# Two fused attention blocks on one core: the seven stores of a prepared weight leave two a step, ahead of a gather

## The chip, the core and the metric

The kernel runs on one NeuronCore of a Trainium2 chip. The metric is the device time of one execution in microseconds (us), of which lower is better. The core has five engines, each with an instruction stream of its own: TensorE (PE), VectorE (DVE), ScalarE (ACT), GpSimd (POOL) and SyncE (SP). SP does no arithmetic here: it issues nearly all transfers between the chip's DRAM and on-chip memory. POOL issues those that add while they move.

## What is computed

Two attention blocks follow each other on x of shape (8, 512, 32, 32) in 32-bit floats; the weights of the two differ. One block, for one batch element with 512 channels C and 1024 positions:

```python
xn = group_norm(x)                       # 8 groups, then gamma and beta
q, k, v = wq @ xn + bq, wk @ xn + bk, wv @ xn + bv     # 512x512 weights
attn = softmax(q^T k * 64 ** -0.5)       # 8 heads of 64 channels, 1024 x 1024
out = x + wp @ (attn v) + bp
```

## The kernel before, in words

**Jobs.** A job is one block on one batch element. There are 16, in the order batch 0 block 0, batch 1 block 0, batch 0 block 1, batch 1 block 1, then the next two batches in the same way. I call them job 0 to job 15. A job has two stages on PE. In the attention, 8 groups (a pair of heads by half of the queries) of 8 steps each follow each other: step i computes one block of scores (`sc`, L1102) and, two steps behind, multiplies an earlier block of exponentials with v (`po`, L1153). In the projections, the output projection of the finished job and v, k and q of the next one are computed (L804, L809; after job 0 the simpler L556 as well).

**Products with seven multiplications.** A matrix product is split in 2x2 blocks and done with seven block products, each on sums of blocks; most projections do this at two levels. The sums of the activations are DVE's work between the attention's steps: L426 to L432 make the sums `t` of xn, and L485 to L491 the second level, in a tile named `deep` (first four steps from xn, last four from `t`). The sums of the weights are made once. For the attention output's and v's weights that is `deep_round`: it loads four raw blocks into a tile `round`, makes four sums of 512 elements a partition and four of 896 with DVE (L165 to L171), and stores seven results of 448 KB each to DRAM (L155). It runs once in each of jobs 0, 1, 2 and 3 (`ROUNDS`). Jobs 0 and 1 also prepare the first level for k and q (`FIRST`, function `put_first`): four loads into a tile `raw`, four sums (again L165 to L171), and two stores to a DRAM tile `keep`. The tiles `round`, `raw` and `deep` take turns in one buffer: the next may be filled only when everything that reads the last, its stores included, is done.

**The softmax's sums.** ACT computes the exponentials `e` (L1107). They are added up by DVE (L1121, L1123), and in most groups the first four of a group go in pairs: POOL issues a transfer that adds one `e` to another (L1130), and DVE adds that sum some steps later (L1133). A sum over partitions follows (r, L1188). After two groups, SP gathers the parts of r (L1211), DVE inverts (lt, ri, rt, L1215 to L1235), SP sends the reciprocals to DRAM (rd, L1228) and back to all partitions (rb, L1230), and DVE multiplies (L1245). Groups also end with a copy-out of `po` (L1174 on ACT, L1176 on DVE). The 12 buffers of `e` serve in the projections for the weights `w`, which SP loads (L192, L198).

**What sets the order.** PE, ACT and DVE run in the order in which the program writes their instructions; transfers marked by `in_turn` keep their place in SP's order. An engine's instruction that waits holds up all that follow it on this engine. In the loop of `run`, each step i issues its scores, values, pair addition, and then what stands under i in two tables: `chores` (DVE work, entered by `put`) and `moves` (mostly transfers, entered by `move`). Both take the next free step if one is taken. A clock that counts planned time (`advance`) starts what `later` has put off, the gather and the inversion among them. In `put_round`, the seven stores go into `moves` from step 26 on at the next free steps, up to the thirties; the gather of r for groups 2 and 3 is issued at about step 34, in between.

Of the kernel before, what the change touches and what calls it, by code (L numbers as in the profile page):

```python
# [54 lines left out]
ROUNDS = {0: (O, 0), 1: (V, 1), 2: (O, 1), 3: (V, 0)}  # L55
# [26 lines left out]
def fast_path(  # L82
# [36 lines left out]
    def advance(us):  # L119
        clock[0] += us  # L120
        due = sorted((t for t in todo if t[0] <= clock[0]), key=lambda t: t[0])
        for t in due:
            todo.remove(t)
            t[1]()
# [956 lines left out]
    class Attention:  # L1081
# [171 lines left out]
            for at, step in zip(times, (gather, invert, spread, normalise)):  # L1253
                later(at, step)

        def run(self, chores, moves, taken=False):


            steps = self.steps
            self.add(1)  # L1260
            self.add(2)
            self.values(0)
            for at in (chores, moves):
                if 2 in at:
                    at[2]()
            for i in range(3, len(steps) + LEAD):
                if i < len(steps):
                    self.scores(i)
                self.values(i - LEAD)
                g, kc = steps[i - LEAD]  # L1270
                if kc % 2 == 1 and kc < 2 * self.pairs(g):
                    self.add_pair(i - LEAD)
                if i in self.due:
                    self.due.pop(i)()
                if kc == NT - 1:
                    if taken and g + 1 == len(self.groups):
                        self.reduce(g)
                    else:
                        self.finish(g)
                    advance(0.85)  # L1280
                for at in (chores, moves):
                    if i in at:
                        at[i]()
                advance(1.71)
# [258 lines left out]
    for n in range(-1, len(jobs)):  # L1543
        last = n + 1 == len(jobs)
        outs = None
        if n >= 0:
            chores, moves = {}, {}

            def put(i, fn):
                while i in chores:  # L1550
                    i += 1
                chores[i] = fn
                return i

            def move(i, fn):
                while i in moves:
                    i += 1
                moves[i] = fn
                return i

            def put_round(which, layer):
                load, first, second, stores = deep_round(which, layer)
                begin = {0: 6, 1: 12}.get(n, 9)
                move(begin, load)
                at = begin + 3
                for fn in first:
                    at = put(at + 1, fn)
                for fn in second:
                    at = put(at + 1, fn)
                at = max(at + 3, 25)  # L1570
                for i, fn in enumerate(stores):
                    at = move(at + 1 + i % 2, fn)

            def put_first(which, layer):
                at = move(37 if n == 0 else 2, lambda: start()) + 3
                box = []

                def start():
                    box.append(acts.tile([P, NW, 2, CH], F32, tag="deep", name=f"raw_{n}"))
                    load_blocks(box[0], layer, which)  # L1580

                for part in range(4):
                    at = put(at + 1, lambda part=part: factor(box[0], part))
                move(at + 1, lambda: store_factors(box[0], layer, which))

            if last:
                w = last_weights(n)
                for part in range(4):
                    put(12 + 2 * part, lambda part=part: factor(w, part))
                for i, fn in enumerate(last_sums(0)):  # L1590
                    put(49 + 3 * i, fn)
            else:
                for i, (_, fn) in enumerate(extra):
                    put(2 + i, fn)
                if n == 1:
                    at = (8, 14, 15, 16, 17, 18, 17, 19, 20, 21)
                else:
                    for i, fn in zip((3, 3, 4, 5, 5, 6, 7, 7, 8), reads):
                        put(i, fn)
                    at = (16, 22, 23, 24, 26, 27, 29, 31, 33, 35)  # L1600
                    if n < DEEP_V + 2:
                        at = (17, 24, 26, 27, 29, 30, 31, 32, 33, 34)
                for i, fn in zip(at[:2], steps):
                    put(i, fn)
                for i, fn in zip(at[2:], steps[2:]):
                    move(i, fn)
                if n == 1:
                    put_first(*FIRST[n])
                for i, fn in zip(at[len(steps) :], sums(n + 1)):
                    put(i, fn)  # L1610
                if n in ROUNDS:
                    put_round(*ROUNDS[n])
                if n == 0:
                    put_first(*FIRST[n])
                put(52 if n in ROUNDS else 48, lambda q=att.q: out_combine(q, None, 0))
                deep_first = deep_steps(n + 1)
                if n + 1 >= DEEP_V:
                    for i, fn in enumerate(deep_first):
                        put(37 + 2 * i if n not in ROUNDS else ((39, 40, 41, 43, 45, 47, 49, 50) if n == 1 else (36, 37, 38, 40, 41, 43, 45, 47))[i], fn)
                else:  # L1620
                    for at, fn in zip((47, 48, 49, 50), deep_first[4:]):
                        put(at, fn)
                move(58, lambda: extend_plan(n + 1))
                for _ in range(RING):
                    move(58, fetch)
            assert max([*chores, *moves], default=0) < NT * len(att.groups) + LEAD
            if n + 1 >= DEEP_V and not last:
                outs = OutputSums(n)
                ahead = deque()
                if jobs[n][1] == 1 and jobs[n][0] + 2 < B:  # L1630
                    ahead.extend(load_steps(jobs[n][0] + 2))
                both, plan_sums = deep_phases(n + 1, ahead, outs)

                att.run(chores, moves, True)
                extra = ahead
                plan_sums()
                banks(0, "one")
                if n + 2 < len(jobs):
                    reads, steps = norm_steps(n + 2)
                att.take(len(att.groups) - 1, both[0])  # L1640
                banks(1, "one")
                for thunk in both[1:]:
                    thunk()
                banks(0, "two")
                att = Attention(n + 1)
                att.scores(0)
                att.scores(1)
                banks(1, "two")
                att.scores(2, "po")
                continue  # L1650
            att.run(chores, moves)
            banks(0, "one")
            banks(1, "one")
            if last:
                for i, fn in enumerate(last_sums(1)):
                    later(7.1 + 0.8 * i, fn)
                later(13.0, judge)
                for sh in range(2):
                    last_proj(n, w, sh)
                break  # L1660
            outs = OutputSums(n)
            out_sums(n, outs)
            first = v_phase(n + 1, ORDER)
            for thunk in first[:-1]:
                thunk()
            rest = first[-1:]
            extra = deque()
            if jobs[n][1] == 1 and jobs[n][0] + 2 < B:
                extra.extend(load_steps(jobs[n][0] + 2))
            if n == 0:  # L1670
                load, bias_steps = make_out_bias(1)
                extra.append((8, load))
                extra.extend((11, fn) for fn in bias_steps)
            if n + 2 < len(jobs):
                reads, steps = norm_steps(n + 2)
                if n + 2 <= DEEP_V:
                    extra.extend((15, fn) for fn in reads)
        both, _ = deep_phases(n + 1, extra, outs, deep_first[:4] if outs else ())
        both[0]()
        rest[0]()  # L1680
        if n < 0:
            later(22.0, lambda: load_x(1))
        for thunk in both[1:]:
            thunk()
        banks(0, "two")
        att = Attention(n + 1)
        att.scores(0)
        att.scores(1)
        banks(1, "two")
        att.scores(2, "po")  # L1690
# [249 lines left out]
```

## Time and profile before

| | |
|---|---|
| median of 3 runs | 3184.72 us (3181.73 to 3185.78) |
| the profiled execution | 3183.33 us |
| its span, first to last instruction | 3181.6 us |
| PE, DVE, ACT, POOL busy | 99%, 83%, 73%, 9% of the span |
| granted PE clock, mean | 0.998 |
| instructions | 62172 |
| DMA | 450.31 MB, 142 GB/s on average |

All readings come from the one profiled execution, in us from the first instruction. A line of a timeline gives the start, the length, engine, source line and operation, the tile written and the tiles read, how many such instructions are merged, and in brackets the idle time before it and what ended it. SPq is SP's queue of transfers; the time there is that of issuing. PE is matrix multiplication, PEld the loading of its weights.

### The profile page before, as it was taken

The numbers are of one execution on the slowest core, as the hardware profiler recorded it, in microseconds if no ns is written. First come the engines' busy times: TensorE is split into PE (matmuls) and PEld (weight loads), VectorE is DVE, ScalarE is ACT, GpSimd is POOL, SyncE is SP. The second block draws the span as 40 slices with busy tenths as digits, with TensorE's granted clock in tenths as the row PEclk, the third lists the DMA queues.
The fourth block names the chain that finished last, engine by engine and source line by source line (L and its number), as shares of the span: only waits on it lengthen the run. The fifth ranks groups of instructions, "written<-read, shape, count | busy, mean of one in ns | idle before, by whom it ended". The sixth has DMA issues, their size and how long they took to land.

```text
span 3181.6 us, 62172 instructions
## 1 busy us (share of the span) xinstructions
PE 3154.0 (99%) x24093; PEld 1875.9 (59%) x24093; DVE 2636.2 (83%) x3571; ACT 2332.2 (73%) x4233; POOL 281.0 (9%) x318
## 2 busy tenths in 40 slices
PE   9999999999999999999999999999999999999999
PEld 8366384563846639466393764837548375573844
DVE  8896898978879788797978969789697887978867
ACT  6648687686877868777686776867768687686864
POOL 0100101011010010100001000010000100001000
PEclk9999999999999999999999999999999999999999
DMA  7555575565735455355554545446456463444733
GB/s 276 140 151 158 137 223 125 149 189 122 240 76 147 117 117 160 75 152 159 144 184 87 158 100 138 125 95 179 131 137 181 90 194 72 130 127 95 222 75 82
DMA packets 186190, 450.31 MB, mean 142 GB/s; under 512 B 37928, under 2 KB 54176, under 8 KB 185888
## 3 DMA queue, kind: packets, MB, share of 16 engines
q1 hardware_dynamic: 137040, 296.82, 27.6%
q0 software_dynamic: 48848, 149.44, 25.8%
q8 instruction: 192, 3.15, 0.4%
q14 instruction: 110, 0.90, 0.1%
HBM read 247.41 MB, written 48.17 MB: 93 GB/s over the span
## 4 chain that ended last, share of the span: by engine, by line
PE 94%; DVE 2%; DMA 2%; issue 1%; ACT 1%; SPq 0%; DVEq 0%; ACTq 0%
PE sc L1102 26%; PE po L1153 26%; PE vd L809 11%; PE zd L809 11%; PE yd L809 5%; PE ud L809 4%; PE vd L804 4%; PE zd L804 3%; PE ud L804 1%; PE yd L804 1%; PE z L556 1%; DVE acc L1123 1%; DMA w<-deep 1%; DMA x<-p 0%; ACT e L1107 0%
## 5 line engine op out<-in xcount | busy, mean ns | idle before, releaser
L1107 ACT ACTIVATE e<-sc 128x1024 f32<-128x1024 f32 x1024 | 1044.2, 1025 | 572.0 <-PE sc L1102 547.8
L1102 PE MATMUL sc<-q,k 64*64 64x512 f32 x8192 | 1058.1, 589 | 0.3 <-ACT e L1107 0.2
L1153 PE MATMUL po<-e,v 64*64 64x512 f32 x8192 | 1057.5, 589 | 0.1
L1153 PEld LDWEIGHTS po<-e,v 64*64 64x64 f32 x8192 | 312.7, 133 | 566.6 <-issue 541.4
L1102 PEld LDWEIGHTS sc<-q,k 64*64 64x64 f32 x8192 | 310.9, 133 | 563.8 <-issue 508.9
L1123 DVE TENSOR_TENSOR acc<-acc,e 128x1024 f32<-128x1024 f32 x320 | 389.5, 1217 | 38.8 <-ACT e L1107 28.4
L1130 POOL DMA_DIRECT2D e<-e x224 | 192.9, 861 | 1756.6 <-ACT e L1107 1362.1
L1121 DVE TENSOR_TENSOR acc<-e,e 128x1024 f32<-128x1024 f32 x128 | 156.4, 1222 | 144.8 <-ACT e L1107 144.7
L1133 DVE TENSOR_TENSOR acc<-acc,e 128x1024 f32<-128x1024 f32 x224 | 272.4, 1216 | 1.8
L809 PE MATMUL zd<-deep,w 128*128 128x256 f32 x860 | 240.2, 379 | 0.0
L809 PE MATMUL vd<-deep,w 128*128 128x256 f32 x804 | 223.5, 379 | 0.0
L809 PEld LDWEIGHTS zd<-deep,w 128*128 128x128 f32 x860 | 163.3, 190 | 22.4 <-ACT ud L504 0.2
L809 PEld LDWEIGHTS vd<-deep,w 128*128 128x128 f32 x804 | 152.8, 190 | 20.8
L1188 DVE TRANSPOSE_TENSOR_REDUCE r<-acc 128x32 f32<-128x1024 f32 x128 | 159.4, 1245 | 4.3
L904 POOL DMA_DIRECT2D x<-p x61 | 72.9, 1195 | 981.0 <-ACT p L826 409.1
L851 DVE TENSOR_TENSOR p<-p,s 128x512 f32<-128x512 f32 x185 | 127.2, 688 | 23.8 <-ACT p L826 18.4
L804 PE MATMUL vd<-w,deep 128*128 128x128 f32 x840 | 120.3, 277 | 1.2 <-ACT ud L504 1.2
L851 DVE TENSOR_TENSOR q<-q,s 128x512 f32<-128x512 f32 x64 | 44.2, 691 | 86.8 <-ACT q L828 45.1
L804 PE MATMUL zd<-w,deep 128*128 128x128 f32 x728 | 107.8, 277 | 1.5 <-ACT ud L504 1.5
L804 PEld LDWEIGHTS vd<-w,deep 128*128 128x128 f32 x840 | 107.0, 193 | 1.9 <-ACT ud L504 1.8
L809 PE MATMUL vd<-os,w 128*128 128x256 f32 x364 | 105.5, 379 | 0.0
L809 PE MATMUL zd<-os,w 128*128 128x256 f32 x356 | 99.0, 379 | 1.7 <-ACT yd L500 1.7
(296 smaller groups left out, 4825.4 us busy)
## 6 DMA issues: line engine op xcount, KB each, us to landing
w<-deep SPq DMA_DIRECT2D x399, 448.0 KB, 5.5
e<-e POOLq DMA_DIRECT2D x224, 512.0 KB, 4.7
x<-p POOLq DMA_DIRECT2D x61, 512.0 KB, 6.5
rb<-rd SPq DMA_DIRECT2D x96, 256.0 KB, 3.9
x<-x_dram SPq DMA_DIRECT2D x28, 512.0 KB, 6.0
out_dram<-x SPq DMA_DIRECT2D x28, 512.0 KB, 5.6
deep<-w SPq DMA_DIRECT2D x28, 448.0 KB, 5.9
deep<-round SPq DMA_DIRECT2D x28, 448.0 KB, 9.0
```

Source lines behind the costliest of these rows:

```text
L804: nc.tensor.matmul(ps[:, tokens], moving[i][:, tokens], lhs[:, FACTOR[i], :], start=(start and ti == 0), stop=True, skip_group_check=True,)
L809: nc.tensor.matmul(ps, lhs[:, FACTOR[i], :], moving[i], start=start, stop=True, skip_group_check=True,)
L851: nc.vector.tensor_add(to_, to_, five.to_broadcast([P, 2, QT]))
L904: nc.gpsimd.dma_start(to_, p(part), accum_op=ALU.add)
L1102: nc.tensor.matmul(sc[h * HD : (h + 1) * HD, j, :], k[r, hp, k0 : k0 + HD], q[r, hp, sh * HALF : (sh + 1) * HALF], start=True, stop=True,)
L1107: nc.scalar.activation(e, sc, AF.Exp, scale=SCALE)
L1121: nc.vector.tensor_add(acc[g], self.es[i - 1], e)
L1123: nc.vector.tensor_add(acc[g], acc[g], e)
L1130: nc.gpsimd.dma_start(self.summed[i], self.summed.pop(i - 1), accum_op=ALU.add)
L1133: nc.vector.tensor_add(self.acc[g], self.acc[g], self.summed.pop(i))
L1153: nc.tensor.matmul(po[g][j * HD : (j + 1) * HD, h, :], v[r, kc, d0 : d0 + HD], e[r, j, :], start=(kc == 0), stop=(kc == NT - 1),)
L1188: nc.vector.tensor_reduce(self.r[:, 0, m, :], self.acc.pop(g).rearrange("p j (b e) -> p (j b) e", e=RP), AX.X, ALU.add, apply_transpose=True,)
```

## The change

The stores get a table of their own, `leaving`, which is read last in each step: two stores a step, in steps 27 to 30 (three pairs and a single one) where the sums are ready by step 26. Steps of `leaving` aren't pushed on by other work. In the built program SP has all seven stores ahead of the gather of groups 2 and 3 in jobs 0 to 3; before, three of them (four in job 1) followed it. Apart from that SP's order is the same.

In job 0 the loads of `raw` are entered at step 35 and not 37, and its four sums by that much sooner; the four `deep` sums from `t` at 46 to 49 and not 47 to 50. In job 1 the eight `deep` sums for the next job are entered at 37, 38, 39, 40, 42, 44, 46, 48 and not at 39, 40, 41, 43, 45, 47, 49, 50. On DVE the order of instructions changes in these two places alone. PE, ACT and POOL keep their order, and no instruction is added or removed.

```diff
--- before.py
+++ after.py
@@ -1253,14 +1253,15 @@
             for at, step in zip(times, (gather, invert, spread, normalise)):
                 later(at, step)
 
-        def run(self, chores, moves, taken=False):
+        def run(self, chores, moves, leaving, taken=False):
 
 
             steps = self.steps
             self.add(1)
             self.add(2)
             self.values(0)
-            for at in (chores, moves):
+            tables = (chores, moves, leaving)
+            for at in tables:
                 if 2 in at:
                     at[2]()
             for i in range(3, len(steps) + LEAD):
@@ -1278,7 +1279,7 @@
                     else:
                         self.finish(g)
                     advance(0.85)
-                for at in (chores, moves):
+                for at in tables:
                     if i in at:
                         at[i]()
                 advance(1.71)
@@ -1544,7 +1545,7 @@
         last = n + 1 == len(jobs)
         outs = None
         if n >= 0:
-            chores, moves = {}, {}
+            chores, moves, leaving = {}, {}, {}
 
             def put(i, fn):
                 while i in chores:
@@ -1567,12 +1568,12 @@
                     at = put(at + 1, fn)
                 for fn in second:
                     at = put(at + 1, fn)
-                at = max(at + 3, 25)
-                for i, fn in enumerate(stores):
-                    at = move(at + 1 + i % 2, fn)
+                at = max(at, 26)
+                for i in range(4):
+                    leaving[at + 1 + i] = lambda part=stores[2 * i : 2 * i + 2]: [fn() for fn in part]
 
             def put_first(which, layer):
-                at = move(37 if n == 0 else 2, lambda: start()) + 3
+                at = move(35 if n == 0 else 2, lambda: start()) + 3
                 box = []
 
                 def start():
@@ -1616,9 +1617,9 @@
                 deep_first = deep_steps(n + 1)
                 if n + 1 >= DEEP_V:
                     for i, fn in enumerate(deep_first):
-                        put(37 + 2 * i if n not in ROUNDS else ((39, 40, 41, 43, 45, 47, 49, 50) if n == 1 else (36, 37, 38, 40, 41, 43, 45, 47))[i], fn)
+                        put(37 + 2 * i if n not in ROUNDS else ((37, 38, 39, 40, 42, 44, 46, 48) if n == 1 else (36, 37, 38, 40, 41, 43, 45, 47))[i], fn)
                 else:
-                    for at, fn in zip((47, 48, 49, 50), deep_first[4:]):
+                    for at, fn in zip((46, 47, 48, 49), deep_first[4:]):
                         put(at, fn)
                 move(58, lambda: extend_plan(n + 1))
                 for _ in range(RING):
@@ -1631,7 +1632,7 @@
                     ahead.extend(load_steps(jobs[n][0] + 2))
                 both, plan_sums = deep_phases(n + 1, ahead, outs)
 
-                att.run(chores, moves, True)
+                att.run(chores, moves, leaving, True)
                 extra = ahead
                 plan_sums()
                 banks(0, "one")
@@ -1648,7 +1649,7 @@
                 banks(1, "two")
                 att.scores(2, "po")
                 continue
-            att.run(chores, moves)
+            att.run(chores, moves, leaving)
             banks(0, "one")
             banks(1, "one")
             if last:
```

## The prediction

> **What bounds the kernel now.** I read the page first, then the stages, then what PE waited for, then the two queues behind those waits.
>
> The page's first part:
>
> ```profile
> PE 3154.0 (99%) x24093; PEld 1875.9 (59%) x24093; DVE 2636.2 (83%) x3571; ACT 2332.2 (73%) x4233; POOL 281.0 (9%) x318
> ```
>
> PE is idle for only 3181.6 - 3154.0 = 27.6 us. The change adds no work and removes none; the built programs have the same instructions on every engine, and PE, ACT and POOL have them in the same order. So it can only win time that PE loses. Where that is shows in the attentions of jobs 0 to 4, cut at the first score matmul and at the first matmul after it (columns: stretch, length, busy time of PE, PEld, DVE, ACT, POOL, clock, DMA share, GB/s):
>
> ```profile
> 79.76:191.65 111.89, 110.19 (x1026) 38.82 (x1025) 95.09 (x124) 73.81 (x77) 13.84 (x15) 1.00 0.61 146
> 284.65:398.65 114.00, 110.56 (x1025) 38.90 (x1025) 93.45 (x112) 73.83 (x77) 12.59 (x15) 1.00 0.58 144
> 486.63:598.12 111.49, 110.11 (x1026) 39.10 (x1025) 96.23 (x119) 73.81 (x77) 13.45 (x15) 1.00 0.56 127
> 687.43:801.83 114.40, 110.33 (x1025) 38.99 (x1025) 97.20 (x120) 73.71 (x77) 13.47 (x15) 1.00 0.55 129
> 888.97:999.00 110.03, 110.03 (x1026) 39.03 (x1025) 92.92 (x113) 73.13 (x76) 12.59 (x15) 1.00 0.49 105
> ```
>
> Job 4 and later ones, which the change doesn't touch, take 110.03. Jobs 0 to 3 lose 1.86, 3.97, 1.46 and 4.37 us. The projections after them, against 85.54 at the end of job 4, lose 2.44 (job 1), 3.77 (job 2) and 1.60 (job 3); after job 0, a shape of its own, PE waits 3.0 and 1.7. All that can be won is about 24 us. PE's waits name the causes (us, times, longest):
>
> ```profile
> PE vd L804 <- DMA w<-deep: 9.2, 4, 4.0
> PE v L556 <- DVE q L1176: 3.0, 1, 3.0
> PE z L556 <- DMA w<-wqkv_dram: 1.7, 1, 1.7
> ```
>
> The 9.2 us lie at the ends of the attentions of jobs 1, 2 and 3. Job 3, from the timelines of SP, DVE and PE:
>
> ```profile
> 736.22 5.19 SPq L155 DMA_DIRECT2D deep<-round  x4
> 752.23 3.42 SPq L1211 DMA_DIRECT2D r<-r  x3
> 755.68 1.72 SPq L155 DMA_DIRECT2D deep<-round  x3
> 791.86 0.33 SPq L1228 DMA_DIRECT2D rd<-rt  x1
> 793.96 1.30 SPq L1230 DMA_DIRECT2D rb<-rd  x2
> 795.42 13.54 SPq L192 DMA_DIRECT2D w<-deep  x11
> ```
>
> ```profile
> 752.12 1.18 DVE L432 TENSOR_TENSOR t<-xn,t 128x1024 f32<-128x1024 f32 x1
> 760.77 1.23 DVE L485 TENSOR_TENSOR deep<-xn 128x1024 f32<-128x1024 f32 x1 [7.46 <-DMA deep<-round]
> 801.83 0.68 PE L804 MATMUL vd<-w,xn 128*128 128x128 f32 x4 [3.96 <-DMA w<-deep]
> ```
>
> Read upwards: PE waits for a weight; its load stands in SP's queue behind the reciprocals' transfer (rd, rb), which waits for DVE's reciprocal; DVE then has no gap back to 760.77, where L485 sat 7.46 us because its tile shares a buffer with the round's; that is free only when all seven stores have landed; and the last three stood behind the gather L1211, which waited until 752.1 for DVE's sum r. The same gap in jobs 0, 1 and 2, at the start of a late run without a pause to the job's end:
>
> ```profile
> 162.25 0.69 DVE L165 TENSOR_TENSOR raw<-raw 128x512 f32<-128x512 f32 x1 [6.33 <-DMA raw<-wqkv_dram]
> 171.22 0.96 DVE L485 TENSOR_TENSOR deep<-t 128x768 f32<-128x768 f32 x1 [1.55 <-DMA keep<-raw]
> 361.58 1.23 DVE L485 TENSOR_TENSOR deep<-xn 128x1024 f32<-128x1024 f32 x1 [4.51 <-DMA deep<-round]
> 559.27 1.23 DVE L485 TENSOR_TENSOR deep<-xn 128x1024 f32<-128x1024 f32 x1 [6.94 <-issue]
> ```
>
> **What the Trainium skill says.** "DMA: Bandwidth & Descriptors", Queues, rings and completion order: each DMA engine goes round the queues that have work, packet by packet. The packet records agree: while a pair's addition (e, 512 KB, POOL's queue) moves, SP's stores get about 0.12 MB/us and the addition lasts 3.5 us; alone the stores move 0.41 MB/us (204 KB per half us). "TensorE: Matmul & The Clock Gate", Part 1: after an idle window of about 3.4 us the array runs at half clock for as long. The clock record agrees: 3.41 us at 0.5 from 399.6 and from 802.4, after idle stretches of 3.17 and 3.96, and none after 1.38 (job 2). So each long wait costs 3.41 / 2 = 1.7 us more. "Perfetto Trace Analysis", Identifying the Most-Contended Engine: matmul busy time is no measure of nearness to the peak; here the 1.60 of projection 3 has no idle in it, so I count stages by their length.
>
> **The change, part by part.** In all four jobs SP now issues seven stores, then the gather. The stores' own waits (the sums of `round`, done by 116.8 in job 0) are over; queued behind them are the gather and, in job 0, the raw loads, so the gather may land later. Its reader, the reciprocal, is no earlier than some 5 us on. What moves is the landing of the last three stores, 3 x 459 KB = 1.38 MB (in job 1 the last four, 1.84 MB). I fill them into what the additions leave.
>
> - Job 3: the first four end at 748.2. Alone until 750.0: 0.73 MB. Beside the first addition, 3.5 us x 0.12 = 0.42. The last 0.22 takes 1.9: 755.4, with 0.4 for the signal 755.8. L485 goes from 760.77 to 755.8: DVE is 5.0 us sooner. The exponentials needed next are ready by 752, so it keeps that to the end. The first weight, 801.7, lands at 796.7, before PE ends at 797.5: the 4.37 go, and with the idle stretch the half clock, 1.60. Together 6.0.
> - Job 2: first four end at 547.6; 1.5 us alone = 0.61, then 0.42, then 0.35 in 2.9: 555.5, with signal 555.9. DVE gains 559.27 - 555.9 = 3.4. Here the next wait is ACT's copy for DVE p L847 (2.8 us) in the projection, which PE feels as 1.5 and 0.8: it moves with DVE, so PE gains 3.4 of its 1.46 + 3.77.
> - Job 1: also the eight sums start two steps sooner, so L485 stands before two acc additions (2.56 us) that used to run ahead of the stall. By 348.4 nearly three stores are through; four are left, 1.87 MB. Beside two additions until 355.4: 0.84; the rest alone 2.5 us: 357.9, signal 358.3. Gain 361.58 - 358.3 - 2.56 = 0.7. The idle stretch falls from 3.17 to 2.5, so I take the half clock to go as well; then p L847 binds 0.9 us later. Net 0.7 + 1.7 - 0.9 = 1.5.
> - Job 0: the three stores: 1.4 us alone 0.57, 0.42, 0.39 in 3.2: landed 149.3. The raw loads, which wait for that, go from 154.03 to 149.3. They took 7.95 us with about 3 lost to an addition: 155.0, not 161.98. But raw L165 now stands before 6.0 us of work that used to precede it (acc, q, lt to rmax, acc, r). Raw's four sums and that work last to 163.6; `keep` lands 4.05 later, 167.6; L485 was at 171.22 with 2.3 us more done. Gain 171.22 - 167.6 - 2.3 = 1.3; I take 1.2. The last q L1176, for which PE waits 3.0 us, moves with it.
>
> Where a moved step costs nothing, its cover is thin. In jobs 0 and 1 a DVE step that waits holds back acc of pair e_33, which frees the buffer of exponential 48: free at about 157.2 against 161.6 needed, and 365.4 against 366.5. A transfer over 4 or 1 us later than I reckon stops ACT and then PE. The copy-out q L1176 has 8 and 4 us. The three t sums moved one step at job 0's end are the same DVE time in another order. Bounds from both ends: if additions always go first, stores land at 150.4, 360.0, 558.3, 758.8: gains 0.1, -1.4, 1.0, 3.6, in all 3.3. If stores go first, the jobs gain at most 2.5, 4.6, 5.2, 6.0: 18.3.
>
> Sum: 1.2 + 1.5 + 3.4 + 6.0 = 12.1 us. The profiled execution took 3183.33 (span 3181.6 and 1.7 around), 1.4 under the median of 3184.72. From the median: 3184.7 - 12.1 = 3172.6.
>
> **Rivals.**
> - Additions win the DMA engines: 3184.7 - 3.3 = 3181.4. For it: an addition slows only from 2.8 to 3.5 us beside stores. Against: stores did get 0.12 MB/us.
> - Stores win, or DVE drains further: 3184.7 - 18.3 = 3166.4. For it: the engines have free stretches between additions. Against: job 1's four stores have none before 355.
> - Weights stay late: the first load took 6.3 us in job 3 against 4.7 in job 1, and rd to rb 3.1 in job 1. If job 3 keeps 4 us of its wait and job 1 gains nothing, 6.6 are left: 3178.1.
> - Slower: the moved DVE steps come before their data. If the stores land no sooner than now, raw L165 in job 0 holds 6.0 us of queued work and L485 in job 1 2.6, and nothing is won in jobs 2 and 3: 3184.7 + 8.6 = 3193.3. It decides below a landing 1.7 us sooner (4 x 1.7 + 1.7 for one half clock = 8.5); I reckon 3.1 to 5.0. For it: thin buffers. Against: SP has nothing before the stores that waits.
> - That the change doesn't do what it says: the built order shows all seven stores before the gather, so only the landing is open.
>
> **How the numbers follow.** Chances: forecast 0.55, stores win 0.17, additions win 0.16, weights late 0.06, slower 0.06. The range, 3167.0 to 3181.5, takes in the forecast and both bounds but for the best end. A difference under about 0.2% (6.4 us) can't be told from none here: faster 0.55 + 0.17 + 0.03 of the late weights = 0.75, same 0.19, slower 0.06.
>
> **What would show it.** Right: L485 in jobs 2 and 3 starts near 556; gaps under 4 us; the attention of job 3 takes 110.0 to 110.5 us; only the start and the end have a half clock; jobs 4 on are unchanged. Wrong: stores land within 1.7 us of now; ACT waits for DVE acc L1133 near 161 or 366; PE's wait for w<-deep stays over 3 us.

## The result, and the profile after

| | before | after |
|---|---|---|
| median of 8 runs each | 3183.09 us (3181.73 to 3185.78) | 3173.19 us (3170.46 to 3176.95) |
| profiled execution, its span | 3183.33, 3181.6 | 3173.06, 3171.3 |

The ratio is 0.9968, with a 95% interval of 0.9957 to 0.9979: faster by 9.9 us, where 12.1 were forecast. The first part of the page of after:

```profile
PE 3151.6 (99%) x24093; PEld 1874.4 (59%) x24093; DVE 2636.1 (83%) x3571; ACT 2333.4 (74%) x4233; POOL 281.1 (9%) x318
```

PE's idle time fell from 27.6 to 3171.3 - 3151.6 = 19.7 us. The stretches of jobs 0 to 3, cut as before (columns as before: stretch, length, busy time of PE, PEld, DVE, ACT, POOL, clock, DMA share, GB/s):

```profile
78.86:192.14 113.28, 110.33 (x1025) 38.99 (x1025) 94.21 (x124) 73.74 (x77) 13.86 (x15) 1.00 0.59 143
285.10:398.75 113.65, 110.79 (x1025) 38.80 (x1025) 92.67 (x111) 73.82 (x77) 12.59 (x15) 1.00 0.59 145
398.75:487.49 88.74, 87.56 (x491) 79.25 (x491) 82.36 (x158) 73.86 (x195) 4.77 (x4) 0.98 0.64 200
487.49:597.51 110.02, 110.02 (x1025) 39.06 (x1024) 99.92 (x122) 73.24 (x76) 13.45 (x15) 1.00 0.59 143
683.18:793.21 110.03, 110.03 (x1025) 38.85 (x1024) 98.14 (x121) 73.25 (x76) 13.47 (x15) 1.00 0.58 140
```

The attentions of jobs 2 and 3 are at the 110.03 of the undisturbed jobs. Job 0's is longer than before (111.89), and in the projection after job 1 the clock column reads 0.98: the half clock is still there. An attention and the projection after it together, and what became of them:

| job | before | after | change | forecast |
|---|---|---|---|---|
| 0 | 204.89 | 206.24 | +1.35 | -1.2 |
| 1 | 201.98 | 202.39 | +0.41 | -1.5 |
| 2 | 200.80 | 195.69 | -5.11 | -3.4 |
| 3 | 201.54 | 196.26 | -5.28 | -6.0 |

The four sum to -8.6. The stretch before the first attention (79.76, now 78.86) and all that follows job 3 each lie another 0.8 to 0.9 lower, though nothing was changed there; that makes up the 10.3 between the two profiled executions. PE's waits after (us, times, longest):

```profile
PE v L556 <- DVE q L1176: 3.5, 1, 3.5
PE vd L804 <- DMA w<-deep: 2.3, 1, 2.3
PE po L1153 <- ACT e L1107: 2.0, 2, 1.7
```

Of the 9.2 us on weights 2.3 are left, all at the end of job 1. New is 1.7 on an exponential, in job 0. SP's timeline around the stores of job 3 (first three lines) and around `keep` in job 0 (last three):

```profile
731.98 9.02 SPq L155 DMA_DIRECT2D deep<-round  x7
747.96 3.11 SPq L1211 DMA_DIRECT2D r<-r  x3
785.23 13.51 SPq L192 DMA_DIRECT2D w<-deep  x11
...
157.78 0.34 SPq L1228 DMA_DIRECT2D rd<-rt  x1
162.60 1.29 SPq L1230 DMA_DIRECT2D rb<-rd  x2
163.98 1.01 SPq L155 DMA_DIRECT2D keep<-raw  x2
```

The seven stores are issued together and the gather follows. The DVE instructions where the stall sits, jobs 0, 0, 1, 2, 3:

```profile
153.31 0.69 DVE L165 TENSOR_TENSOR raw<-raw 128x512 f32<-128x512 f32 x1 [4.87 <-DMA raw<-wqkv_dram]
169.94 0.96 DVE L485 TENSOR_TENSOR deep<-t 128x768 f32<-128x768 f32 x1 [5.89 <-DMA keep<-raw]
360.16 1.23 DVE L485 TENSOR_TENSOR deep<-xn 128x1024 f32<-128x1024 f32 x1 [5.91 <-issue]
553.20 1.22 DVE L485 TENSOR_TENSOR deep<-xn 128x1024 f32<-128x1024 f32 x1
750.29 1.23 DVE L485 TENSOR_TENSOR deep<-xn 128x1024 f32<-128x1024 f32 x1 [1.25 <-DMA deep<-round]
```

In jobs 2 and 3 the gaps of 6.94 and 7.46 are gone or down to 1.25. In job 1 the gap grew from 4.51 to 5.91, and in job 0 both add up to 10.8, from 7.9. So the gain of jobs 2 and 3 is the whole gain, and jobs 0 and 1 give a little back. My theory after this: the stores ahead of the gather help in all four jobs, and the DVE steps that the change moves in jobs 0 and 1 cost there about as much as the stores win, since they now stand ahead of their data. The rival: early stores do nothing for jobs 0 and 1 (additions or the gather take the DMA engines), and the moved steps are harmless.

### The profile page after: what moved, and what is told of

It is laid out like the page before. It is cut to its first block, busy times and chain, and to the rows that moved or that the text cites. A ratio compares the mean times of both kernels' runs of the same rounds, so it can differ in the third digit from the quotient of the medians.

```text
span 3171.3 us, 62173 instructions
## 1 busy us (share of the span) xinstructions
PE 3151.6 (99%) x24093; PEld 1874.4 (59%) x24093; DVE 2636.1 (83%) x3571; ACT 2333.4 (74%) x4233; POOL 281.1 (9%) x318
## 4 chain that ended last, share of the span: by engine, by line
PE 92%; DVE 4%; DMA 1%; issue 1%; SPq 0%; ACT 0%; DVEq 0%; POOL 0%; ACTq 0%; POOLq 0%
PE sc L1102 25%; PE po L1153 25%; PE vd L809 11%; PE zd L809 11%; PE yd L809 5%; PE ud L809 4%; PE vd L804 4%; PE zd L804 3%; PE ud L804 1%; PE yd L804 1%; DVE acc L1123 1%; PE z L556 1%; DVE acc L1133 1%; DMA keep<-raw 0%; DVE r L1188 0%
## 5 line engine op out<-in xcount | busy, mean ns | idle before, releaser
L1121 DVE TENSOR_TENSOR acc<-e,e 128x1024 f32<-128x1024 f32 x128 | 156.5, 1223 | 147.6 <-ACT e L1107 147.5
L1133 DVE TENSOR_TENSOR acc<-acc,e 128x1024 f32<-128x1024 f32 x224 | 272.6, 1217 | 1.8
```

What stands on the lines that cost most here:

```text
L1121: nc.vector.tensor_add(acc[g], self.es[i - 1], e)
L1133: nc.vector.tensor_add(self.acc[g], self.acc[g], self.summed.pop(i))
```

## The experiments

**The stores alone.** After, with the DVE steps of jobs 0 and 1 back where they were. DVE's order is that of before (step 39 for the raw loads of job 0 is what gives this order), SP's that of after.

```diff
-                at = move(35 if n == 0 else 2, lambda: start()) + 3
+                at = move(39 if n == 0 else 2, lambda: start()) + 3
...
-   ((37, 38, 39, 40, 42, 44, 46, 48) if n == 1 else ...
+   ((39, 40, 41, 43, 45, 47, 49, 50) if n == 1 else ...
...
-                    for at, fn in zip((46, 47, 48, 49), deep_first[4:]):
+                    for at, fn in zip((47, 48, 49, 50), deep_first[4:]):
```

> The stores go two a step ahead of the gather in jobs 0 to 3, and DVE keeps the order of before in jobs 0 and 1. Theory (the whole gain is the stores' earlier landing; the moved DVE steps stand ahead of their data and cost): job 0 wins about 4 us against before instead of losing 1.4, job 1 about 2.8 instead of losing 0.4, jobs 2 and 3 about 10 as in the changed kernel: some 3165 us where the changed kernel has 3173. Rival (the earlier sums in jobs 0 and 1 are a part of the gain): 3173 or more.

Measured: 3166.2 us (3164.16 to 3167.9), ratio to before 0.9941 [0.9927, 0.9955]: 18 us faster than before and 7 faster than after. The stretches of its jobs 0 to 3 (attention only):

```profile
80.40:190.43 110.03, 110.03 (x1026) 39.09 (x1025) 96.71 (x126) 73.17 (x76) 13.82 (x15) 1.00 0.63 154
281.94:393.07 111.13, 110.56 (x1025) 38.90 (x1025) 92.17 (x111) 73.43 (x77) 12.58 (x15) 1.00 0.59 147
482.21:592.24 110.03, 110.03 (x1026) 39.06 (x1025) 99.65 (x122) 73.19 (x76) 13.45 (x15) 1.00 0.60 144
678.08:788.11 110.03, 110.03 (x1026) 39.06 (x1025) 98.20 (x121) 73.18 (x76) 13.46 (x15) 1.00 0.59 140
```

With the projections, jobs 0 to 3 take 201.54, 200.27, 195.87 and 196.18: the stores alone win 3.4, 1.7, 4.9 and 5.4. Jobs 0 and 1 thus fell short of the 4 and 2.8 expected. The clock record shows half speed at the end alone. No version that does all the work was faster.

**The sums alone.** Before, with job 1's eight sums two steps sooner and nothing else.

```diff
-   ((39, 40, 41, 43, 45, 47, 49, 50) if n == 1 else ...
+   ((37, 38, 39, 40, 42, 44, 46, 48) if n == 1 else ...
```

> Before, with job 1's eight deep sums two steps sooner and nothing else. Theory: the first sum waits as before until 361.6, now with two acc additions (2.56 us) queued behind it, and job 1's end comes 2.6 us later: 3186 against 3183, PE's wait for w<-deep there near 5.7 us. Rival (sums that start sooner finish sooner): 3181 to 3182.

Measured: 3186.57 us, ratio to before 1.0008 [0.9999, 1.0016]. The total alone can't tell this from no change; the stage can: job 1's attention takes 116.31 instead of 114.00, near the 2.6 expected. PE's wait for the weight there came to 3.34 and not 5.7; another 1.24 went to a wait for an exponential. DVE's timeline shows why:

```profile
361.08 1.23 DVE L485 TENSOR_TENSOR deep<-xn 128x1024 f32<-128x1024 f32 x1 [7.17 <-DMA deep<-round]
```

The stall is 7.17 instead of 4.51. It ends when it did (76.7 us after the attention's start, before 76.9), so the two acc additions that used to run ahead of the stall, 2.5 us, now run after it.

**Job 0 back, and job 1 back.** After with one half of the DVE moves undone: in the first, job 0's raw loads go to step 39 and the sums from `t` to 47 to 50; in the second, job 1's sums go to 39 to 50. The lines are those of the first experiment's diff.

> The changed kernel with job 0's raw blocks and four sums back where they were; job 1's sums stay sooner. Theory: job 0 wins some 5 us against the changed kernel, 3168 against 3173. Rival: 3173 or more.

> The changed kernel with job 1's eight sums back where they were; job 0's steps stay sooner. Theory: job 1 wins some 3 us against the changed kernel and its half-clock stretch goes, 3170 against 3173. Rival: 3173 or more.

Measured: 3169.98 us both times, ratios to before 0.9955 [0.9941, 0.9969] and 0.9959 [0.9946, 0.9973]; each is 3.2 under after. Each interval reaches over 4 us to both sides, so the stages carry the reading, not the medians. In the first, job 0 takes 110.03 + 91.49 = 201.52 (after 206.24) and job 1 stays at 202.7. In the second, job 1 takes 110.94 + 88.74 = 199.68 (after 202.39) with no half clock behind it, and job 0 stays at 205.2. The first wins 4.7 in job 0 and the second 2.7 in job 1: each loss belongs to its own job's moved steps. The projection after job 1 is no shorter for the full clock, though: 88.74 in the second and in after alike. In the second PE waits there 1.39 and 1.09 for ACT's copy-outs (ud, L504), in after 1.09 for one of them.

**No additions.** After, with the pair transfers of groups 3 and 4 left out in jobs 0 to 3, which are those beside the stores.

```diff
-            nc.gpsimd.dma_start(self.summed[i], self.summed.pop(i - 1), accum_op=ALU.add)
+            if self.n in ROUNDS and g in (3, 4):
+                self.summed.pop(i - 1)
+            else:
+                nc.gpsimd.dma_start(self.summed[i], self.summed.pop(i - 1), accum_op=ALU.add)
```

> The changed kernel, but in jobs 0 to 3 the transfers that add a batch's pairs in DRAM (groups 3 and 4 of the scores) are left out; VectorE adds what has been written later alone, so those scores lack half of their pairs. Theory (in job 1 the stores lie beside the additions, and the last of them is what L485 waits for): with no addition beside them seven stores of 2.75 MB at 0.41 MB/us take 6.7 us, they land near 352 to 354 in the trace's time, L485 starts near 354 instead of 360.2 and has no wait on the transfers, the projection of job 1 starts some 3 to 4 us sooner in the job, and the PE wait on w<-deep of 2.3 us goes. In job 0 the gather sets the raw loads, so little changes there beyond the rd and rb pair that go faster: L485 near 166. Total 3166 to 3168. Rival (the additions cost nothing: the stores' own length and the two accs behind the step set job 1): L485 stays at 359 to 361 and the total at 3173.

The transfers left out add one tile `e` to another on chip, not in DRAM as the expectation says, and the seven stores are 3.21 MB and not 2.75.

Measured: 3166.83 us, ratio to before 0.9947 [0.9933, 0.9961]. Job 1 as expected and more: 110.76 + 86.12 = 196.88, 5.5 under after, no wait on w<-deep left. Its SP and its DVE:

```profile
337.88 0.35 SPq L1231 DMA_DIRECT2D rd<-rt  x1
339.28 1.31 SPq L1233 DMA_DIRECT2D rb<-rd  x2
343.51 6.05 SPq L155 DMA_DIRECT2D deep<-round  x7
```

```profile
354.99 1.23 DVE L485 TENSOR_TENSOR deep<-xn 128x1024 f32<-128x1024 f32 x1 [1.40 <-issue]
```

L485 stands 69.1 us after the attention's start (354.99 - 285.90); in after 75.1. So in job 1 the additions hold the stores up by 6 us. The 1.40 still left is a wait for the stores, though the view says issue: a transfer's semaphore counts to 16 in the trace, and for the seventh store fifteen counts are in by 352.86 and the last at 354.82. Also rb follows rd by 1.4 us here and by 4.5 in after. Job 0 missed the expectation: L485 at 168.79 and not 166, with a stall of 5.99, and the job takes 206.0 as in after. The additions left out are not what ails job 0. But those of the next group remain: POOL issues two there, at 154.51 and 157.94, beside rd and rb, so this experiment doesn't tell what they cost job 0, and the expectation that rd and rb go faster there overlooked them.

**`keep` from another queue.** After, with the two keep stores of job 0 issued by POOL.

```diff
-            in_turn(keep[:, s], w[:, s])
+            if (which, layer) == FIRST[0]:
+                tc.keep_in_program_order(nc.gpsimd.dma_start(keep[:, s], w[:, s]))
+            else:
+                in_turn(keep[:, s], w[:, s])
```

> The changed kernel, with the two keep stores of job 0 issued from POOL's queue rather than SP's. Theory (keep was late since it stood behind rd and rb in SP's queue, which wait for a transfer and its landing): keep lands at 165 to 166, L485 of job 0 starts near 166 instead of 169.9, ACT's waits for acc near 175 and 189 go or shrink below 1 us, attention of job 0 falls from 113.3 to 110.0 to 111, total 3169 to 3170.5. Rival (the DMA engines are full with the pair additions at that time, and keep would be late from any queue): L485 stays at 169 to 170 and the total at 3173.

Measured: 3171.78 us, ratio to before 0.9963 [0.9949, 0.9977]; that is 1.4 under after, less than expected and within the noise. Job 0 itself goes as the theory has it: the timeline of DVE at this sum of `deep` (L488 in this kernel, whose later lines are shifted by three) and that of POOL:

```profile
167.13 0.96 DVE L488 TENSOR_TENSOR deep<-t 128x768 f32<-128x768 f32 x1 [2.72 <-DMA keep<-raw]
```

```profile
162.25 1.11 POOL L177 DMA_DIRECT2D keep<-raw  x2 [7.71 <-DVE raw L171]
163.35 0.92 POOL L1133 DMA_DIRECT2D e<-e  x1
```

The stall falls from 5.89 to 2.72, ACT no longer waits for acc, the attention takes 110.79 instead of 113.28, and the job 203.50 instead of 206.24. But PE's wait for q is still 3.0, with the half clock behind it, and the projections of jobs 2 and 3 came out 1.4 and 0.5 longer in this execution. And it is not a clean cut: `keep` on POOL also holds back the second pair addition until 163.35, so that rd travels without one beside it: SP has rd at 158.15 and rb at 159.54. Whether `keep` gained from leaving SP's queue or from that addition's delay isn't separated.

DVE's two stalls in job 0 (at raw and at keep) against the job's length put all of this side by side:

| kernel | stalls | job 0 |
|---|---|---|
| stores alone | 0 + 3.4 = 3.4 | 201.5 |
| job 0 back | 0 + 3.4 = 3.4 | 201.5 |
| keep from POOL | 5.1 + 2.7 = 7.8 | 203.5 |
| before | 6.3 + 1.6 = 7.9 | 204.9 |
| no additions (groups 3, 4) | 3.4 + 6.0 = 9.4 | 206.0 |
| job 1 back | 4.7 + 5.0 = 9.8 | 205.2 |
| after | 4.9 + 5.9 = 10.8 | 206.2 |

## Why the prediction was right, and where it was not

The total, the sign and the leading mechanism held: the last stores moved ahead of the gather, land sooner, and release L485. The parts held less well than the sum: jobs 0 and 1 came out 4.5 us worse than forecast, jobs 2 and 3 together 1.0 better. By the profiles the four jobs won 8.6; a gain of 9.9 so near to 12.1 owes something to stretches that the change doesn't touch. That is luck. Of the signs named, the attention of job 3 held (110.03), L485 in jobs 2 and 3 ran as soon as named or sooner, and what follows job 3 changed by 0.8 us. Two failed: gaps of 5.9 are left in jobs 0 and 1, and the projections behind these two attentions still have a stretch at half clock each.

**Job 3, step right.** L485 was to come 5.0 us sooner; counted from the attention's start it came 73.34 - 67.11 = 6.2 sooner. The attention's 4.37 went as forecast. Of the projection's 1.60, all put down to the half clock, only 0.91 went, though the half clock is gone. Of the rest 0.42 is a wait of PE at 808.22, again for ACT's ud L504; what the remainder is stays open.

**Job 2, step right in kind, a term mis-sized.** L485 was to come 3.4 sooner and came 6.9 sooner, with no wait left; PE won 5.11 of the 5.23 that it could lose. The wrong term is "1.5 us alone = 0.61, then 0.42, then 0.35 in 2.9": I let the additions begin at their old times and left the stores 0.12 MB/us beside them. The DMA view of after in the stretch 548 to 552 (queue, packets, MB, share) shows otherwise:

```profile
q1 hardware_dynamic: 476, 1.48, 91.3%
q0 software_dynamic: 28, 0.11, 14.3%
```

POOL issued the additions at 548.37 and 551.80, and the stores (q1) went on at their full rate until 551.3; only then, at 551.34, did the first addition (q0) start to move, 3.0 us after its issue. In before, with the stores through by 547.5, the addition issued at 547.51 moved at 548.9, after 1.4 us. In job 3 of after it is the same: issued at 744.06, moving from 747.11. So on this stretch the rival "stores win" described what happened. The Trainium skill, "DMA: Bandwidth & Descriptors", Queues, rings and completion order, which has each DMA engine take the queues in turn packet by packet, doesn't foretell this: while the stores ran, the addition got 0.11 MB of 1.59. What holds an addition back at its start no run here settles.

**Job 1, wrong.** The landing came later than reckoned ("the rest alone 2.5 us: 357.9, signal 358.3"): L485 ran at 360.16, which counted from the attention's start is 1.9 sooner than before, and not 3.3. With the 2.56 us of acc that I had put behind the stall DVE was 0.7 us late where I had a gain of 0.7. By the packet records the bulk of the stores is through at 357, as reckoned, but the last 0.03 MB trickles in until 359.9. Of the seventh store's sixteen counts fifteen are in at 358.03 and the last at 359.98: 1.95 us of the lateness hang on the last of the sixteen. The additions don't explain that lag, since one of 1.96 is there without them too (352.86 to 354.82); in before there is none (361.33 and 361.36), and what causes it stays open. The additions did win for a while: they began to move at 350.5, before the stores were through, and left them 0.06 MB/us at first, not 0.12; without them L485 runs 6 us sooner. And "I take the half clock to go as well" failed twice. PE's wait of 2.31 still had one behind it. And once the sums are put back and the half clock is gone, the projection is as long as with it. So the 1.7 that I put on it, less 0.9 for p L847, was not there to be won as long as ACT's copy-outs come late. Without the additions, where PE waits only 0.31 for them, the projection takes 86.12.

**Job 0, wrong in sign.** The loads step was right: raw L165 runs 8.0 us sooner in the job, forecast 7.0. The failing term is "`keep` lands 4.05 later": from the end of raw's last sum (160.93, 0.65 long) to L485 it took 169.94 - 161.58 = 8.4 us. In before, rb had been issued 5.0 us ahead of `keep`, and was through. Now rd goes out at 157.78 beside two additions, rb can follow only at 162.60, and `keep` leaves SP 1.4 us after it and moves from 166 on, behind rb's packets. I counted what queues behind the raw loads on DVE and not that their sums had now caught up with rd and rb on SP. How much of this is the order on SP and how much the two additions beside rd stays open: the experiment on the queue changed both, and the one without additions left these two in (8.5 us there as well). The stores alone give a hint. There rb is out at 155.33, `keep` leaves at 161.79, at once after raw's last sum, and L485 still runs 6.6 us after that sum (161.76 to 168.34), beside an addition. So 4.05 was too short even with nothing ahead of `keep` on SP. DVE's last q L1176, counted from the attention's start, is then 1.9 us later than before (121.44 against 119.55).

**The thin cover, foreseen as a risk.** The text named a stop of ACT at acc L1133, near 161 or 366, if a transfer came late. It came in job 0, but later: 1.47 us at 175.26. The larger wait, 3.01 at 188.76, is for acc L1121, which the text didn't name (before has 1.12 there). ACT's waits from 140 to 205 of after:

```profile
ACT e L1107 <- DVE acc L1121: 3.0, 1, 3.0
ACT e L1107 <- DVE acc L1133: 1.5, 1, 1.5
```

PE then waits 1.74 at 189.84 for the exponential, which is the new line in its waits and by itself more than job 0's loss of 1.35. The half clock that follows PE's wait for q in after seems to add nothing to the job: before has 1.7 us there in which PE waits for ACT's yd, and these are gone.

**The rivals.** "Slower: the moved DVE steps come before their data" was right as a mechanism in jobs 0 and 1, and near in size there: by the stages the moved steps cost 4.7 and 2.7 us, where it has 6.0 and 2.6. What it has wrong is that nothing is won in jobs 2 and 3. The cost is more than the stores win in these jobs (3.4 and 1.7); the gain of jobs 2 and 3 covers it. Most of the 18.3 us that I allowed when stores go first was there to be had: stores alone gives 15.4 in jobs 0 to 3 by its profile. That the medians give 18.3 as well (3184.51 to 3166.2) is chance, since their interval runs from 14 to 23. The change gives away some 7 of it by its second half.

## What to carry to other kernels

When a change does two things, price them by themselves: here issuing the stores ahead of a waiting transfer won 18 us, and starting the readers sooner to go with it lost 7. A step that waits for a transfer should be moved forward on an in-order engine only by as much as its data move, counted at the landing: every microsecond of other work that it passes is taken away from the time in which that transfer was hidden. And the landing has to be counted over again for each queue that the step's own transfers now meet (here `keep`, caught behind rd and rb).

## What the runs showed of the hardware

- An accumulating transfer that is issued while a run of stores streams at 0.41 MB/us starts late: in after its first packet moves 3.0 to 3.1 us after issue in jobs 0, 2 and 3 and 3.8 in job 1, against 1.4 where no stores move. Once it moves it takes the larger share: 0.17 MB/us against 0.06 for the stores from 351 to 353 (job 1 of after).
- A transfer of 8 KB (rd) takes several times as long beside additions. From its issue to that of rb, which waits for it, 1.4 us pass where no addition moves, 2.7 beside one (job 0 of the kernel without additions in groups 3 and 4), and 4.5 and 4.8 beside two (jobs 1 and 0 of after). In the last three rb goes 0.2, 0.2 and 0.4 us after an addition issued ahead of rd has landed (159.06, 341.51, 162.18). It isn't always so: at 761.62 of after rb goes 2.9 us after rd, 1.8 before the second of two additions has landed.
- The half clock doesn't follow from the length of a wait: after 2.31 us of idle PE (job 1 of after) there was one, after 2.98 (job 0 of before) none, and after 2.96 (keep from POOL) one. In the prediction I took a threshold between 1.38 and 3.17 from three cases, and on the length there is none. The clock records show what decides. The stretches at half clock are one or two times 3.413 us long, and within a run they start whole multiples of 3.413 us apart: in before at 399.63 and 802.40, 118 apart; in after at 200.53 and 398.51, 58 apart. So there are windows at fixed times. Laid over PE's idle time in all eight traces, leaving out the first 20 us and the end, they give one rule without an exception: from full clock, a half clock followed each of the eleven windows in which PE was idle for 62% or more, and none of those with 53% or less. The 2.98 us in before fall into two windows, 34% and 53%; in after the 2.31 us and a wait of 0.28 just ahead of it fill 68% of one. The Trainium skill, "TensorE: Matmul & The Clock Gate", Part 1, says that the window of about 3.4 us is free-running, which the record bears out, and that the half clock follows an idle one; here a window idle for 62% was enough. Whether a wait of 2 to 3 us costs a half clock thus depends on where it falls.
